# Four-layer graph network on one core: the scatters of layers 1 and 3 become one 128x128 matmul per slot tile

## Chip, core and metric

The kernel runs on one core of one Trainium2 chip. The metric is the device time of one execution in microseconds. The time before is the median of three executions, 5735.22 us, with 5725.06 us the lowest and 5747.24 us the highest.

## What is computed

A graph of 12,500 nodes and 200,000 edges, sorted by destination, passes through four layers. Each layer's result is added to its input and normalised over the 96 features of a node. Cut to the parts that move data over the edges:

```python
x = _layernorm(x + L0(x))   # mean over the edges into a node of x[src], two weight matrices
x = _layernorm(x + L1(x))   # twice: segment_sum((x @ W0 + b0)[src], dst), joined with x @ W1 + b1, times W2, divided by its std
x = _layernorm(x + L2(x))   # attention with 8 heads: exp(clip(sum(K[src] * Q[dst] * E(edge_attr)))) weighs V[src]
x = _layernorm(x + L3(x))   # softmax over the edges into a node: ex = exp(m), sum(ex * m) / sum(ex), then one matrix
```

So each layer gathers a row for every edge by its source and sums the rows by destination. L1 does this twice (depth 2), and L3 sums two quantities for each edge.

## The kernel before

The nodes are 98 tiles of 128. Edges are handled in two ways.

For the first destination tiles (`NS` = 72 tiles in layers 0 and 1, `NS3` = 64 tiles in layer 3) edges are placed in *slots*: each destination tile has `SQ` = 25 slot tiles of 128 slots, and a slot tile is made of four *granules* of `GR` = 32 slots, each of which draws its rows from one source tile. Two one-hot matrices in fp8 belong to a destination tile: `ohT` (source node by slot) and `ohd` (slot by destination node). A slot tile is worked off in three steps:

- *gather* (L1389): four matmuls, one for each granule, each with 128 rows and 32 columns of weights, write the 128 gathered rows into PSUM (`rows1`, `rows2`). A gathered row has `W` numbers: 192 in layers 0 and 1 (a value as two fp16 halves), 384 in layer 3;
- *copy* (L1392): ScalarE or VectorE copies them to SBUF as fp16 (`msg1`, `msg2`);
- *scatter* (L1399): four matmuls, each with 32 columns of `ohd` as weights and the same copied rows as moving operand, add to the 32-partition quarters of one accumulator `acc`, over the 25 slot tiles of a destination tile.

For the remaining destination tiles the rows are fetched straight from DRAM by GpSimd's indirect DMAs, 128 rows each (L1334, into a ring of `rows_e` tiles), and summed by one matmul per edge tile and destination tile, with a one-hot matrix `ones_e` of 128x128 that VectorE makes (L1315, L1320). The helper `by_edges` does this, and its `take(d)` issues the 32 matmuls of a destination tile.

The program has five parts in time. The first (L0, `first_sums`, with its own gather and scatter at L1251 and L1265) also builds the one-hot matrices and stores them. Two calls of `whole_pass` follow, one for each depth of L1, then the attention (`attention`, L1560 to L1700), then a third call of `whole_pass` for L3. A call of `whole_pass` goes through its slot tiles in groups of `5 * R` (10 in L1, 5 in L3, as `R = 4 * D // W`): it gathers a group in three pieces, two copied by ScalarE and one by VectorE, then scatters the group before, and after each group takes from `by_edges` its proportional share. When four destination tiles are complete a stage function runs (`l1_stage` with transposes at L747 and matmuls at L1463 or L1511; `l3_stage` with L1747 to L1777 and matmuls at L1767).

This is the order in which the code calls the steps. The order in which instructions stand on each engine is made from it by a scheduler that has its own costs for the instructions; inside an engine they run in that order. In `whole_pass` PSUM holds two `acc` buffers, one buffer of `rows1` and two of `rows2`. SBUF holds four buffers each of `msg1` and `msg2`, three of each one-hot matrix, and a ring of 16 (L1) or 13 (L3) `rows_e` tiles of four edge tiles each.

Calls of `whole_pass`: `whole_pass(rest, tabs_d[1 + i], ...)` for i = 0, 1 inside `passes()`, and `whole_pass(at_3, ex_d, ...)` after `attention()`. Together they scatter 2 x 72 x 25 = 3,600 slot tiles of 192 columns and 64 x 25 = 1,600 of 384 columns.

Of the kernel before, what the change touches and what calls it, by code (L numbers as in the profile page):

```python
# [23 lines left out]
P = 128  # L24
# [491 lines left out]
GR = 32  # L516
NG = 4
SQ = 25
# [23 lines left out]
def gnn_fast(  # L542
# [4 lines left out]
    nc = tc.nc  # L547
# [630 lines left out]
    def reload(work, d, bufs=3):  # L1178
        o = work.tile([P, SD], FP8, name="ohT0", bufs=bufs)
        nc.sync.dma_start(o, ohT_d[d])  # L1180
        ohd = work.tile([P, SQ, P], FP8, name="ohd", bufs=bufs)
        nc.sync.dma_start(ohd.rearrange("p q e -> p (q e)"), ohd_d[d])
        return o, ohd

    def load_table(pool, table):

        pieces, at = new_table(pool, table.shape[1], F16)
        for k, t in enumerate(pieces):
            (nc.sync, nc.scalar)[k % 2].dma_start(t, rows(table, k * CT, t.shape[1]))
        return at  # L1190
# [10 lines left out]
    def gather_spares(pool, table, d):  # L1201

        t = pool.tile([P, table.shape[1]], F16, name="spare", bufs=4)
        nc.gpsimd.indirect_dma_start(
            out=t, out_offset=None, in_=table,
            in_offset=bass.IndirectOffsetOnAxis(ap=spare_2[:, d // 2 : d // 2 + 1], axis=0),
        )
        return t

    def granule(at, ohs, sp, q, j, half=0):  # L1210

        if q == SQ - 1 and j < 2:
            c = half * SPARE + j * GR
            return ident_h[:, c : c + GR], sp
        s = NG * q + j - (2 if q == SQ - 1 else 0)
        return ohs[:, q * P + j * GR : q * P + (j + 1) * GR], at(s)
# [131 lines left out]
    def whole_pass(of, table, done, rest_done, at=None):  # L1348

        ns = of[0]  # L1350
        W = table.shape[1]
        R = 4 * D // W
        items = [(d, q) for d in range(ns) for q in range(SQ)]
        got, acc = {}, {}
        with ExitStack() as c2:
            tabp = c2.enter_context(tc.tile_pool(name="e_tab", bufs=1))
            work = c2.enter_context(tc.tile_pool(name="e_work", bufs=2))
            msgp = c2.enter_context(tc.tile_pool(name="e_msg", bufs=4))
            psum = c2.enter_context(tc.tile_pool(name="e_psum", bufs=1, space=PSUM))
            at = at or load_table(tabp, table)  # L1360
            sp = {}

            def ask_spares(d):
                if d < ns:
                    sp[d] = sp[d + 1] = gather_spares(tabp, table, d)

            ask_spares(0)
            ask_spares(2)
            others = by_edges(of, msgp, psum, work, table, rest_done, 16 if W == 2 * D else 13)
            next(others)  # L1370
            made = 0

            def fetch(d):
                if d < ns:
                    if d % 2 == 0:
                        ask_spares(d + 4)
                    got[d] = reload(work, d)

            def gather(now, banks, engine):

                n = len(now) // R
                ps = psum.tile([P, n, 512], F32, name=f"rows{n}", bufs=n)
                m = msgp.tile([P, n, R * W], F16, name=f"msg{n}")
                for i, (d, q) in enumerate(now):
                    if q == 0:
                        fetch(d + 1)
                    for j in range(NG):
                        a, b = granule(at, got[d][0], sp[d], q, j, d % 2)
                        nc.tensor.matmul(  # L1389
                            ps[j * GR : (j + 1) * GR, i // R, i % R * W : (i % R + 1) * W], a, b, start=True, stop=True  # L1390
                        )
                (nc.scalar.copy if engine else nc.vector.tensor_copy)(m, ps[:, :, : R * W])  # L1392
                return [(d, q, m[:, i // R, i % R * W : (i % R + 1) * W]) for i, (d, q) in enumerate(now)]

            def scatter(d, q, m):
                if q == 0:
                    acc[d] = psum.tile([P, 512], F32, name="acc", bufs=2)
                for j in range(0, P, GR):
                    nc.tensor.matmul(  # L1399
                        acc[d][j : j + GR, :W], got[d][1][:, q, j : j + GR], m, start=(q == 0), stop=(q == SQ - 1)  # L1400
                    )
                if q == SQ - 1:
                    done(work, psum, d, acc.pop(d))
                    got.pop(d)
                    sp.pop(d)

            fetch(0)
            waiting = []
            for i in range(0, len(items), 5 * R):
                now = []  # L1410
                for b0, b1, scalar in ((0, 1, True), (1, 3, True), (3, 5, False)):
                    now += gather(items[i + b0 * R : i + b1 * R], b1 - b0, scalar)
                for w in waiting:
                    scatter(*w)
                waiting = now
                while made * len(items) < i * 4 * (NB - ns):
                    next(others)
                    made += 1
            for w in waiting:
                scatter(*w)  # L1420
            for _ in others:
                pass
# [491 lines left out]
```

## Time and profile before

| | |
|---|---|
| median of three executions | 5735.22 us |
| the profiled execution | 5735.91 us |
| its span (first to last instruction) | 5733.9 us |
| mean granted TensorE clock | 0.773 |
| TensorE matmuls busy (PE) | 4175.5 us, 73%, 72,859 instructions |
| TensorE weight loads busy (PEld) | 3370.6 us, 59%, 72,859 instructions |
| VectorE (DVE) / ScalarE (ACT) / GpSimd (POOL) busy | 4365.7 / 2727.9 / 3866.0 us |
| L1399, the scatters of the change | 756.2 us of PE busy time, 20,800 matmuls |
| L1389, the gathers of the same passes | 796.5 us, 20,384 matmuls from the tables |
| the two passes of L1 | about 1480 to 2125 us and 2125 to 2800 us of the span |
| the pass of L3 | about 4866 to 5734 us |

Busy times of an engine are the union of its instructions, and matmuls are pipelined: an instruction's own duration (277 ns on average at L1399) is much longer than the distance to the next. "issue" as the reason of an idle time means that the engine waited for no semaphore that the profile shows. In rows of instructions, `128*32` is rows by columns of the array in use, and `xN` a count.

### The profile page before, as it was taken

How to read it: one execution, taken by the hardware profiler on the slowest of the kernel's cores; microseconds unless marked ns; L12 is line 12 of the kernel's file. 1: busy time of each engine (PE TensorE's matmuls, PEld its weight loads, DVE VectorE, ACT ScalarE, POOL GpSimd, SP SyncE). 2: the span in 40 equal slices, each digit the busy share in tenths (PEclk: the TensorE clock that was granted, in tenths of full speed). 3: DMA queues.
4: the chain of work that ended last, by engine and by line, in shares of the span. 5: the costliest groups of instructions: out<-in, count | busy, mean ns of one | idle time of the engine just before them, and what ended most of it. 6: DMA issues, size and time to landing. Idle time of an engine off the chain costs nothing. (4 is left out here: it accounts for less than half of the span.)

```text
span 5733.9 us, 175104 instructions
## 1 busy us (share of the span) xinstructions
PE 4175.5 (73%) x72859; PEld 3370.6 (59%) x72859; DVE 4365.7 (76%) x10305; ACT 2727.9 (48%) x5420; POOL 3866.0 (67%) x3587
## 2 busy tenths in 40 slices
PE   4657766676678877787667677667667666899998
PEld 2545555555567666666466666566666665566665
DVE  7589999998466656666578888888888787677777
ACT  1445555556344434444444545544554454455454
POOL 0267676777577747776277777777777776776663
PEclk7677877888899989999765656655665565999999
DMA  4556666665655645666455555555555554455553
GB/s 103 150 179 198 190 202 199 199 198 177 162 162 166 167 130 161 175 177 173 131 156 159 159 158 161 159 160 159 161 159 161 157 158 131 140 155 149 143 145 90
DMA packets 670059, 920.37 MB, mean 161 GB/s; under 512 B 398170, under 2 KB 463437, under 8 KB 669253
## 3 DMA queue, kind: packets, MB, share of 16 engines
q1 hardware_dynamic: 503350, 624.83, 34.9%
q0 software_dynamic: 147648, 277.89, 19.3%
q8 instruction: 573, 9.39, 0.7%
q10 hardware_dynamic: 18255, 6.35, 0.5%
q14 instruction: 233, 1.91, 0.1%
HBM read 775.87 MB, written 132.81 MB: 158 GB/s over the span
## 5 line engine op out<-in xcount | busy, mean ns | idle before, releaser
L1334 POOL DMA_INDIRECT rows_e<-tab_d,cols x1257 | 1556.3, 1238 | 472.6 <-issue 289.8
L1560 POOL DMA_INDIRECT kv<-kv_d,cols x1563 | 1546.3, 989 | 484.6 <-issue 380.2
L1392 ACT CAST msg<-rows 128x384 f16<-128x384 f32 (+1 forms) x1360 | 820.2, 639 | 784.1 <-PE rows L1389 758.9
L1652 PE MATMUL acc<-mh,ohe 128*128 128x208 f16 x3115 | 561.5, 353 | 623.4 <-DVE ohe L1638 621.5
L1392 DVE CAST msg<-rows 128x768 f16<-128x768 f32 x680 | 649.5, 955 | 387.6 <-PE rows L1389 373.2
L1389 PE MATMUL rows<-tab,ohT 128*32 128x192 f16 (+1 forms) x20384 | 796.5, 277 | 155.4 <-issue 51.8
L1399 PE MATMUL acc<-msg,ohd 128*32 128x192 f16 (+1 forms) x20800 | 756.2, 277 | 70.5 <-issue 65.2
L1652 PEld LDWEIGHTS <-ohe 128*128 128x128 bf16 x3115 | 359.0, 129 | 758.4 <-DVE ohe L1638 702.9
L1389 PEld LDWEIGHTS <-ohT 128*32 128x32 fp8e4 x20384 | 515.0, 98 | 327.6 <-issue 253.1
L1598 PE MATMUL ep<-w_e,attr 97*128 97x96 f32 x3126 | 690.5, 396 | 5.0 <-DVE s L1606 4.2
L1334 POOL DMA_INDIRECT rows_e<-ex_d,cols x547 | 530.6, 970 | 215.5 <-issue 138.7
L1598 PEld LDWEIGHTS ep<-w_e,attr 97*128 97x128 f32 x3126 | 660.8, 311 | 13.4 <-DVE s L1606 4.6
L1399 PEld LDWEIGHTS <-ohd 128*32 128x32 fp8e4 x20800 | 520.8, 99 | 186.4 <-issue 110.0
L1618 ACT ACTIVATE ex<-sc 128x32 f32<-128x32 f32 x391 | 89.6, 229 | 935.4 <-DVE sc L1610 913.1
L1320 PE MATMUL acc<-rows_e,ones_e 128*128 128x192 f16 (+2 forms) x3532 | 464.4, 282 | 84.0 <-DMA rows_e<-tab_d,cols 30.1
L1255 ACT CAST msg<-rows 128x768 f16<-128x768 f32 x600 | 361.3, 640 | 306.2 <-PE rows L1251 283.4
L1606 DVE TENSOR_TENSOR s<-ep,kv 128x384 f32<-128x384 f32 x391 | 217.6, 557 | 310.7 <-DMA kv<-kv_d,cols 230.4
L1320 PEld LDWEIGHTS <-ones_e 128*128 128x128 bf16 x3532 | 338.2, 117 | 189.4 <-issue 98.7
L1265 PE MATMUL acc<-msg,ohd 128*32 128x193 f16 x7200 | 332.8, 287 | 132.2 <-ACT msg L1255 124.7
L1251 PE MATMUL rows<-tab,ohT 128*32 128x192 f16 x7056 | 336.5, 286 | 34.8 <-DVE ohT L1174 12.6
L1638 DVE TENSOR_SCALAR ohe<-wide,within 128x256 bf16<-128x256 bf16 x1563 | 359.5, 314 | 0.0
L1031 DVE TENSOR_TENSOR_SCAN cnt<-cb,run,sb 128x2048 bf16<-128x2048 bf16 (+1 forms) x73 | 324.6, 4447 | 3.7 <-DMA cb<-crow 3.6
(703 smaller groups left out, 7252.9 us busy)
## 6 DMA issues: line engine op xcount, KB each, us to landing
ohT<-ohT_d SPq DMA_DIRECT2D x208, 400.0 KB
ohd<-ohd_d SPq DMA_DIRECT2D x208, 400.0 KB
attr<-cols_edge_attr_dram SPq DMA_DIRECT2D x390, 192.0 KB
bc<-rowd SPq DMA_DIRECT2D x72, 800.0 KB
qb<-qrow SPq DMA_DIRECT2D x97, 512.0 KB
sb<-srow SPq DMA_DIRECT2D x72, 512.0 KB
cb<-crow SPq DMA_DIRECT2D x72, 512.0 KB
ohd_d<-ohd SPq DMA_DIRECT2D x72, 400.0 KB
```

The source lines that it names most:

```text
L1251: nc.tensor.matmul(ps[j * GR : (j + 1) * GR, i // R, i % R * W : (i % R + 1) * W], a, b, start=True, stop=True)
L1255: nc.scalar.copy(m[:, : n * R, :W].rearrange("p (b r) w -> p b r w", r=R), ps[:, :n, : R * W].rearrange("p b (r w) -> p b r w", r=R),)
L1265: nc.tensor.matmul(acc[d][j : j + GR, : W + 1], got[d][1][:, q, j : j + GR], m, start=(q == 0), stop=(q == SQ - 1))
L1320: nc.tensor.matmul(acc[:, : W + count], ones[:, :, i], rows_of[u][:, i, : W + count], start=(t + i == first), stop=(t + i == last),)
L1334: nc.gpsimd.indirect_dma_start(out=m[:, i, :W], out_offset=None, in_=table, in_offset=bass.IndirectOffsetOnAxis(ap=rest_src[:, t : t + 1], ...
L1389: nc.tensor.matmul(ps[j * GR : (j + 1) * GR, i // R, i % R * W : (i % R + 1) * W], a, b, start=True, stop=True)
L1392: (nc.scalar.copy if engine else nc.vector.tensor_copy)(m, ps[:, :, : R * W])
L1399: nc.tensor.matmul(acc[d][j : j + GR, :W], got[d][1][:, q, j : j + GR], m, start=(q == 0), stop=(q == SQ - 1))
L1560: nc.gpsimd.indirect_dma_start(out=kv[:, i, :], out_offset=None, in_=kv_d, in_offset=bass.IndirectOffsetOnAxis(ap=cols[:, t0 + i : t0 + i ...
L1598: nc.tensor.matmul(ep[:, i, :], a[:, i * P : (i + 1) * P], w_e, start=True, stop=True)
L1638: nc.vector.tensor_scalar(o[:, i], wide, within[:, t0 + i : t0 + i + 1], None, op0=ALU.is_equal)
L1652: nc.tensor.matmul(acc[d].rearrange("p t w -> p (t w)"), ohe[:, i, k * P : (k + 1) * P], m[:, i].rearrange("p t w -> p (t w)"), start=(t = ...
```

## The change

In `whole_pass` the four scatter matmuls of a slot tile, one for each 32-column group, become one matmul with the whole 128x128 block of `ohd` as weights, which writes all 128 partitions of `acc`. The gathers in the same passes still use 32 columns at a time, and `first_sums` keeps its four scatters.

```diff
             def scatter(d, q, m):
                 if q == 0:
                     acc[d] = psum.tile([P, 512], F32, name="acc", bufs=2)
-                for j in range(0, P, GR):
-                    nc.tensor.matmul(
-                        acc[d][j : j + GR, :W], got[d][1][:, q, j : j + GR], m, start=(q == 0), stop=(q == SQ - 1)
-                    )
+                nc.tensor.matmul(acc[d][:, :W], got[d][1][:, q, :], m, start=(q == 0), stop=(q == SQ - 1))
                 if q == SQ - 1:
                     done(work, psum, d, acc.pop(d))
```

## Prediction

> **What bounds the kernel now.** I read the page first, then the engines' busy time by part of the program, the groups of instructions of each pass by form, and the timeline of TensorE inside the passes. The profiled execution took 5735.91 us, 2.0 us more than its span and 0.7 us more than the median, so sums are made against 5735.9 and carry over to the median less 0.7. A measurement of this kernel can tell about 0.5% (29 us) from no change.
>
> ```profile
> span 5733.9 us, 175104 instructions
> PE 4175.5 (73%) x72859; PEld 3370.6 (59%) x72859; DVE 4365.7 (76%) x10305; ACT 2727.9 (48%) x5420; POOL 3866.0 (67%) x3587
> ...
> q8 instruction: 573, 9.39, 0.7%
> ```
>
> No engine bounds the whole. By part (engines' busy us and counts, granted clock, DMA share, GB/s):
>
> ```profile
> 0.00:1480.00 1480.00, 956.31 (x18293) 744.18 (x18293) 1265.23 (x2768) 717.99 (x1334) 870.41 (x534) 0.77 0.59 179
> 1480.00:2125.00 645.00, 500.70 (x15685) 433.36 (x15689) 374.00 (x785) 273.83 (x539) 446.36 (x461) 0.92 0.56 156
> 2125.00:2800.00 675.00, 518.31 (x15347) 416.34 (x15335) 438.31 (x949) 300.20 (x669) 441.57 (x450) 0.94 0.58 163
> 2800.00:4866.00 2066.00, 1409.50 (x9394) 1260.36 (x9394) 1654.38 (x4612) 1012.73 (x2140) 1546.86 (x1564) 0.59 0.55 158
> 4866.00:5734.00 868.00, 790.72 (x14153) 516.40 (x14152) 633.76 (x1193) 423.16 (x741) 560.83 (x579) 0.97 0.48 136
> ```
>
> Rows two, three and five are the changed passes. In L3 PE is busy 791 of 868 us. In L1 it is busy 78%, and POOL's 461 operations matter. The groups of the first pass of L1 (first three lines) and of L3 (last four):
>
> ```profile
> L1334 POOL DMA_INDIRECT rows_e<-tab_d,cols x423 | 409.9, 969 | 129.6 <-issue 111.2 <-PE rows L1389 6.1 <-DMA rows_e<-tab_d,cols 5.2
> L1389 PE MATMUL rows<-tab,ohT 128*32 128x192 f16 x7174 | 220.9, 255 | 50.8 <-issue 24.3 <-DMA ohd<-ohd_d 9.8 <-DVE msg L1392 6.6
> L1399 PE MATMUL acc<-msg,ohd 128*32 128x192 f16 x7252 | 213.1, 256 | 39.1 <-issue 39.1
> ...
> L1334 POOL DMA_INDIRECT rows_e<-ex_d,cols x547 | 530.6, 970 | 215.5 <-issue 138.7 <-PE acc L1320 56.7 <-PE rows L1389 15.2
> L1389 PE MATMUL rows<-tab,ohT 128*32 128x384 f16 x6252 | 356.9, 329 | 40.6 <-ACT msg L1392 20.6 <-DVE msg L1392 18.2
> L1399 PE MATMUL acc<-msg,ohd 128*32 128x384 f16 x6400 | 339.4, 328 | 5.3 <-DVE msg L1392 5.3
> L1320 PE MATMUL acc<-rows_e,ones_e 128*128 128x384 f16 x1075 | 191.6, 330 | 19.2 <-DMA rows_e<-ex_d,cols 18.5 <-DVE ones_e L1315 0.6
> ```
>
> In L3 POOL waits 56.7 us for PE's `acc`: it is ahead, and PE sets the pass. In the first pass of L1 POOL waits for hardly anything but its own issue, 0.3 us after each 0.97 us operation; 461 of them need 585 of the 645 us, so POOL sets the pace and PE barely keeps up. In the second pass POOL waits 15.8 us for `acc`, so PE leads there, by little.
>
> **What a slot tile costs in either form.** TensorE alone, in L3 and then L1 (start, us, count):
>
> ```profile
> 5101.56 0.67 PE L1399 MATMUL acc<-msg,ohd 128*32 128x384 f16 x12
> 5102.05 0.35 PE L1389 MATMUL rows<-tab,ohT 128*32 128x384 f16 x4
> 5102.33 0.84 PE L1320 MATMUL acc<-rows_e,ones_e 128*128 128x384 f16 x4
> 5103.10 0.35 PE L1389 MATMUL rows<-tab,ohT 128*32 128x384 f16 x4
> ...
> 1627.15 0.59 PE L1389 MATMUL rows<-tab,ohT 128*32 128x192 f16 x17 [0.65 <-issue]
> 1627.49 1.07 PE L1399 MATMUL acc<-msg,ohd 128*32 128x192 f16 x40
> 1628.32 1.07 PE L1389 MATMUL rows<-tab,ohT 128*32 128x192 f16 x40
> 1629.14 0.83 PE L1399 MATMUL acc<-msg,ohd 128*32 128x192 f16 x31
> 1631.17 0.42 PE L1399 MATMUL acc<-msg,ohd 128*32 128x192 f16 x9 [1.20 <-issue]
> ...
> 1661.36 2.83 PE L1320 MATMUL acc<-rows_e,ones_e 128*128 128x192 f16 x32
> ```
>
> The 12 scatters of 5101.56 are three slot tiles, and the next group starts 0.49 us later: 0.163 us a slot tile. The full matmuls of 5102.33 take 0.84 us for four; less 0.33 us for the last one's own length, 0.17 us each. In L1 ten slot tiles take 0.83 us (1627.49 to 1628.32), and 32 full matmuls (2.83 - 0.25) / 31 = 0.083 us each. So the four column groups already run side by side, and four of them cost what one full matmul costs. **The change saves no streaming time.** That is the first step, and it denies the change its plainest gain.
>
> **What is added: changes of shape.** From the four gathers at 5102.05 to the full matmul is 0.28 us instead of 0.163: +0.12. The four full ones lose another 0.03, as the first weights of the new shape load uncovered. Their last starts at 5102.33 + 0.84 - 0.33 = 5102.84, and the next gathers at 5103.10: 0.26, so +0.10. There and back costs 0.25 us, 0.12 us a change. The Trainium skill (TensorEngine Tiling, Tiling Modes) has it as a rule that changing the tiling mode, not only the tile, drains TensorE; the rows agree, and it gives no price.
>
> In the built programs' orders on PE, the first stage and the attention are the same instructions in the same order. The three passes go from 196, 264 and 172 changes between 32-column and wider matmuls to 459, 559 and 875: in L3 395 from gather to scatter and 359 back, as its 1,600 scatters stand mostly in runs of five. Added are 263, 295 and 703, times 0.12: 32, 35 and 84 us of TensorE time.
>
> **What is removed: instructions.** Every slot tile loses three weight loads and three matmuls, 5,200 x 6 = 31,200 of PE's 145,718. Their time was shared with the fourth, so they cost only where instructions run short. There they do: at 1627.15 and 1631.17 TensorE stands still inside a run, waiting for "issue". Between the two stand 17 + 40 + 40 + 31 = 128 matmuls with as many loads, and the page's instruction queue q8 moved 9.39 MB in 573 packets, 145,718 / 573 = 254 instructions to a packet. I read this as PE running out of fetched instructions: 256 of them last 32 x 0.083 = 2.7 us but came after 4.0 us. The PE rows of L1 put 39.1 + 24.3 = 63 us on issue in the first pass and 26.1 + 27.5 = 54 us in the second; those of L3 none, where 256 instructions last 32 x 0.163 = 5.2 us. After the change a group of L1 is 80 instructions of gather and 20 of scatter in 0.83 + 0.83 + 0.25 = 1.9 us, so 256 last 4.9 us, longer than 4.0. The bounds are nothing saved and all 117 us; near the upper end, I take 85%: 54 and 46 us.
>
> **The sum.** First pass of L1: 32 - 54 = -22 us for PE, but POOL's 585 us stand, and PE can win only part of the 60 us around them: -10. Second pass: 35 - 46 = -11, kept, since POOL waits there. L3: +84, on the engine that sets the pass. Some of it falls where PE waits anyway: its matmul rows wait 40.6 + 5.3 + 18.5 = 64 us for copies and rows, and a PE 10% slower finds these sooner ready. I take a third, 20: +64. No other queue is moved past anything that counts; SP's and POOL's work is the same in number. Together +43: 5735.9 + 43 = 5779, **5778 us** against the median. Its own range goes from L3 covered by half of those waits (84 - 32 - 21 = +31) to nothing covered and half of the stalls left (84 + 67 - 58 = +93): 5766 to 5828.
>
> **Rivals.**
> *Covered drains, faster.* If changes of shape fall where PE waits for copies, rows or instructions anyway, L1 shows only the removed stalls, -10 (POOL) and -46, and L3 84 - 64 = +20: -36, 5699 us. It decides from the point where a change costs L3 less than (56 - 29) / 703 = 0.04 us. For it: 64 us of waits in L3. Against: PE is some 95% busy between 5000 and 5650 us, and L3's waits lie in bursts around its stages, the changes in every group.
> *They cancel.* L3 at half its price, +42, and L1 at -21: +21, 5756 us.
> *The stalls stay.* If a fetch is late because of what other queues move (DMA share 0.56), not because PE is quick, L1 pays 67 and gains nothing: 67 + 84 = +151, 5886 us; cover could take 20 off. Against it: L3, at the same DMA share within 0.1, has none.
> *The quarter matmuls are not quite parallel.* If each group of four cost more than one full matmul, the change would save on all 5,200 slot tiles. A run of 20 in L3 takes 1.00 us; less 0.33 and four distances of 0.163, 0.02 us remain, and a run of 12 (0.67) leaves the same 0.01 to 0.02, so it is paid once in a run. Paid on every slot tile it would be 5,200 x 0.02 = 104 us, 32 of them in L3, and in L1, with POOL's pace, about 20 of the rest: 43 - 52 = -9, 5726 us. The Trainium skill (TensorE: Matmul & The Clock Gate, Part 3) gives such a span, the matmul's length and about 4 ns for each further tile; by it 12 ns x 5,200, an estimate of 62 us, would be saved in place of 104. The rows speak against paying it on each.
>
> **How the numbers follow.** Forecast 0.54, stalls stay 0.08: slower 0.62. They cancel 0.18, not quite parallel 0.05: within 0.5%, 0.23. Covered drains: faster 0.15. The range leaves out the far half of the faster case and nearly all of the stalls' case: 5705 to 5835.
>
> **What would show it.** Right: in L3 PE's distances inside runs stay 0.163 us, weight loads at both ends of each scatter run wait about 0.1 to 0.2 us for issue, and the pass grows by some 64 us; the issue waits of 1.2 us in L1 are nearly gone and POOL's 1.27 us beat fills the first pass as before; L0 and attention keep their length. Wrong: L3 grows by under 30 us (cover), or L1 still shows stalls inside runs of gathers.

## The result, and the profile after

The changed kernel is faster: 5694.09 us in the median of four executions (5689.09 to 5701.9) against 5735.93 us for the kernel before beside it, a ratio of 0.9929, with a 95% interval of 0.9912 to 0.9946. On another chip, in four executions, it took 5690.28 us where the kernel before took 5735.41 us, a ratio of 0.9914 (0.9897 to 0.9932). The prediction was 5778 us, slower than before, with a range from 5705 to 5835: the time moved the other way and lies below the range. The profiled execution took 5689.09 us.

From the page of the changed kernel, the lines that answer to those shown of before:

```profile
span 5687.3 us, 143915 instructions
PE 4272.4 (75%) x57259; PEld 3233.5 (57%) x57259; DVE 4359.9 (77%) x10305; ACT 2734.2 (48%) x5420; POOL 3876.0 (68%) x3587
...
q8 instruction: 451, 7.39, 0.5%
```

TensorE is busy 97 us *longer* (4272.4 against 4175.5) with 15,600 matmuls fewer, and the kernel is 47 us shorter: time that was idle has gone. By part of the program (the columns are those of the same view of before: stretch, length, busy us and count of PE, PEld, DVE, ACT and POOL, granted clock, DMA share, GB/s):

```profile
0.00:1480.00 1480.00, 964.10 (x18293) 749.43 (x18293) 1263.46 (x2764) 717.76 (x1334) 878.03 (x533) 0.76 0.60 179
1480.00:2100.00 620.00, 512.53 (x10173) 411.54 (x10177) 373.22 (x787) 273.36 (x536) 441.20 (x459) 0.91 0.60 160
2100.00:2735.00 635.00, 543.77 (x10072) 400.95 (x10061) 433.64 (x956) 307.83 (x679) 447.97 (x454) 0.94 0.65 177
2735.00:4805.00 2070.00, 1416.21 (x9550) 1259.43 (x9551) 1662.98 (x4618) 1019.44 (x2147) 1557.78 (x1573) 0.59 0.57 158
4805.00:5687.00 882.00, 835.74 (x9187) 412.13 (x9183) 626.56 (x1181) 415.76 (x726) 551.03 (x570) 0.97 0.48 132
```

From here on a pass is measured from its first scatter to its last, read from the start times in the trace. The first pass of L1 went from 611 to 586 us, the second from 657 to 600, L3 from 844 to 871: -25, -57 and +27. L0 and the attention are within 5 us of what they were. The groups of the first pass of L1 (two lines) and of L3 (three), by form:

```profile
L1334 POOL DMA_INDIRECT rows_e<-tab_d,cols x420 | 404.6, 963 | 128.0 <-issue 108.8 <-DMA rows_e<-tab_d,cols 9.1 <-PE rows L1389 5.8
...
L1398 PE MATMUL acc<-msg,ohd 128*128 128x192 f16 x1800 | 190.1, 253 | 0.0
...
L1334 POOL DMA_INDIRECT rows_e<-ex_d,cols x541 | 523.9, 968 | 237.1 <-issue 134.3 <-PE acc L1320 80.9 <-PE rows L1389 16.4
...
L1389 PE MATMUL rows<-tab,ohT 128*32 128x384 f16 x6118 | 343.6, 330 | 12.7 <-ACT msg L1392 11.8 <-DVE msg L1392 0.2
L1398 PE MATMUL acc<-msg,ohd 128*128 128x384 f16 x1570 | 323.1, 329 | 0.0
```

In L1 the 39.1 us that the scatters waited for issue are gone, as predicted. In L3 TensorE waits less for copies (by its waits over the whole pass 18.0 us, 38.8 before), and POOL waits 80.9 us for `acc` where it waited 56.7: TensorE sets that pass more firmly than before. TensorE alone, in L1 and then in L3 (start, us, count):

```profile
1626.40 1.01 PE L1389 MATMUL rows<-tab,ohT 128*32 128x192 f16 x40
1627.34 1.00 PE L1398 MATMUL acc<-msg,ohd 128*128 128x192 f16 x10
1628.27 1.01 PE L1389 MATMUL rows<-tab,ohT 128*32 128x192 f16 x40
...
5054.02 1.00 PE L1389 MATMUL rows<-tab,ohT 128*32 128x384 f16 x20
5054.95 0.99 PE L1398 MATMUL acc<-msg,ohd 128*128 128x384 f16 x5
5055.87 0.35 PE L1389 MATMUL rows<-tab,ohT 128*32 128x384 f16 x4
```

A group of L1 (ten slot tiles gathered, ten scattered) takes 1628.27 - 1626.40 = 1.87 us with no stall in it; 1.9 was predicted. A group of L3 takes 5055.87 - 5054.02 = 1.85 us where ten distances of 0.163 make 1.63: 0.22 us for the drains (the time lost at a change of shape) there and back, where 0.25 was predicted. These mechanisms are all there, which points to something that the sum did not hold.

### The profile page after: what moved, and what is told of

Its sections match the earlier page's. It is cut to its first block, busy times and chain, and to the rows that moved or that the text cites. A ratio compares the mean times of both kernels' runs of the same rounds, so it can differ in the third digit from the quotient of the medians.

```text
span 5687.3 us, 143915 instructions
## 1 busy us (share of the span) xinstructions
PE 4272.4 (75%) x57259; PEld 3233.5 (57%) x57259; DVE 4359.9 (77%) x10305; ACT 2734.2 (48%) x5420; POOL 3876.0 (68%) x3587
## 5 line engine op out<-in xcount | busy, mean ns | idle before, releaser
L1334 POOL DMA_INDIRECT rows_e<-tab_d,cols x1257 | 1576.9, 1255 | 457.8 <-issue 290.4
L1389 PE MATMUL rows<-tab,ohT 128*32 128x192 f16 (+1 forms) x20384 | 780.7, 277 | 61.9 <-ACT msg L1392 18.6
L1398 PE MATMUL acc<-msg,ohd 128*128 128x192 f16 (+1 forms) x5200 | 708.3, 276 | 1.4 <-issue 1.3
L1389 PEld LDWEIGHTS <-ohT 128*32 128x32 fp8e4 x20384 | 432.0, 97 | 366.6 <-issue 314.5
L1398 PEld LDWEIGHTS <-ohd 128*128 128x128 fp8e4 x5200 | 413.1, 99 | 241.8 <-issue 183.8
```

Source lines behind the costliest of these rows:

```text
L1334: nc.gpsimd.indirect_dma_start(out=m[:, i, :W], out_offset=None, in_=table, in_offset=bass.IndirectOffsetOnAxis(ap=rest_src[:, t : t + 1], ...
L1389: nc.tensor.matmul(ps[j * GR : (j + 1) * GR, i // R, i % R * W : (i % R + 1) * W], a, b, start=True, stop=True)
L1398: nc.tensor.matmul(acc[d][:, :W], got[d][1][:, q, :], m, start=(q == 0), stop=(q == SQ - 1))
```

## The experiments: the matmul, or the order

The change does two things at once. It replaces four instructions by one, and it gives the scheduler another cost for the scatter, so that all five engines get another order of instructions. The prediction took the new order from the built program, but only to count changes of shape in it. One theory: *the form* of the matmul makes the result (fewer stalls in L1, drains that are better hidden). The other: *the order* makes the gain, because waits inside TensorE's order become shorter, and the form costs about what was predicted. To part them, the order of one kernel was forced on the other, instruction by instruction on every engine in the three passes, by dependencies that carry no semaphore (`...` stands for lines left out, here and below):

```diff
+    for engine in (ET.PE, ET.DVE, ET.Activation, ET.Pool, ET.SP):
+        own = [i for i in traced[a:b] if i.engine == engine and type(i).__name__.startswith("Inst")]
+        ...
+        for step in given[at : at + len(own)]:
+            k += step
+            if last is not None:
+                tc.add_manual_dep(own[k], last.name, mybir.DependencyInfo(
+                    mybir.DependencyClass.NoSync, mybir.DependencyReason.DATA), reason="order")
+            last = own[k]
```

`one_old` is the changed kernel in the order of before; `four_new` is the kernel before (four matmuls, kept together) in the order of after. The traces bear the edit out: VectorE, ScalarE and GpSimd have the same operations in the same order in `one_old_c` as in the kernel before, and in `four_new_d` as in the changed kernel. Beside them the change was made in one layer alone, the scheduler free to order (`l1_only`, shown against the changed kernel; `l3_only` has `R == 1` in place of `R == 2`):

```diff
-                nc.tensor.matmul(acc[d][:, :W], got[d][1][:, q, :], m, start=(q == 0), stop=(q == SQ - 1))
+                G = P if R == 2 else GR
+                for j in range(0, P, G):
+                    nc.tensor.matmul(
+                        acc[d][j : j + G, :W], got[d][1][:, q, j : j + G], m, start=(q == 0), stop=(q == SQ - 1)
+                    )
```

Some of these runs were on two chips on which the kernel before takes 8058 and 8066 us; they are told first and kept apart.

**On the slower chips.** Kernel `one_old`:

> One 128x128 matmul per slot tile, but every engine in the three passes is held to the order of instructions of the kernel before. Instruction supply and cover (the theory): the time comes from fewer instructions in L1 and from drains that L3's waits cover, whatever the order: 5685 to 5705 us, the two L1 passes 40 us or more shorter together, L3 about 27 us longer. Order (rival): the gain is the scheduler's new order, which puts the stages' transposes later behind the scatters; without it the waits stay: L1 shorter by no more than 30 us together, L3 longer by 60 to 80, 5765 to 5785 us.

Kernel `four_new`:

> Four quarter matmuls per slot tile as before, but every engine in the three passes is held to the order of the changed kernel. Supply and cover: the instructions are as many as before and the stalls stay, 5725 to 5745 us, issue waits of PE in L1 near 117 us. Order: the waits at the transposes go and there are no drains, so L1 shorter by 30 us and L3 by 50: 5645 to 5670 us.

The change in layer 1 alone, and in layer 3 alone:

> One matmul per slot tile in the two passes of L1, four in L3. If the parts add up (both theories): L1 as in the changed kernel, 75 to 85 us shorter, L3 as before: 5655 to 5670 us. If the slower L3 of the changed kernel came from something that it inherits from L1: L3 stays 27 us longer, 5690 us.

> Four matmuls in L1, one in L3. If the parts add up: L1 as before, L3 27 us longer: 5755 to 5770 us. If the drains of L3 are wholly covered when it starts from the state that the old L1 leaves: 5735 us.

Measured against 8058.47 us: `one_old_order` 8014.54 (ratio 0.9945, 0.9925 to 0.9965), `four_new_order` 8018.41 (0.9961, 0.9947 to 0.9974), `l1_only` 7950.23 (0.9871, 0.9849 to 0.9894), `l3_only` 8089.97 (1.0056, 1.0036 to 1.0076). The form alone and the order alone both gain here, by some 40 us each. Numbers of us for a pass can't be held against these runs, since the passes of L1 take about 1,000 us in place of 600. The sign by layer holds: layer 1 gains, layer 3 loses. On the second of these chips, with one kernel more (strict turns in L3, below):

> One 128x128 matmul per slot tile in the order of the kernel before (looked at part by part this time). Supply and cover: the two passes of L1 about 75 us shorter together than before's 1268, L3 about 27 us longer than 844. Order: L1 30 us shorter at most, L3 60 to 80 us longer. Both at work, each with about half, as the slower chip showed it: L1 40 us shorter, L3 15 to 20 us longer.

> Four quarter matmuls in the order of the changed kernel. Supply and cover: L1 1268 us as before with issue waits near 117 us, L3 844 us. Order: L1 30 us shorter, L3 50 us shorter. Both: L1 35 to 40 us shorter, L3 10 us longer.

> One matmul in L1, four in L3. If the parts add up, L1 1186 us as in the changed kernel and L3 844 us as before: 5660 us in all.

> The changed kernel with one thing more: in L3 the groups of five gathers and of five scatters are held in strict turns, which takes the changes of shape in L3 from 876 to 715. If each drain stands on PE's path at 0.105 us, L3 is 17 us shorter than the changed kernel's 871: 854. If the drains lie in waits, it stays at 871; if the fixed turns make PE wait for copies, it is longer.

Against 8065.7 us, one execution each: 8029.79, 8024.0, 7974.11 and 7959.99 us. The first three repeat the times above within 24 us. The copies take as long here as in `l1_only_c`, the same kernel on a faster chip (800 ns on ScalarE and 955 on VectorE for 128x768, against 800 and 954); TensorE is what differs. Its waits in `l1_only_b` over the whole span (engine, line, waited for, us, times, longest):

```profile
PE rows L1389 <- issue: 605.0, 750, 3.2
...
PE acc L1400 <- issue: 298.4, 391, 2.5
```

750 and 391 times it stood still without a semaphore, for 0.8 us on average; in the profile of before the same two lines have some 50 such stalls each. With fewer instructions in L1 the kernel gains there (`l1_only`), but with fewer in L3 it still loses (`l3_only`). What slows these chips is open, and no result below rests on them.

**On chips where the kernel before takes 5731 to 5749 us.**

> One matmul per slot tile in the order of the kernel before, for a chip where before takes 5735 us; by parts, before being L1 611 + 657 and L3 844, after 586 + 600 and 871. Supply and cover, whatever the order: L1 1186 as after, L3 871. Order alone: L1 1240 or more, L3 905 to 925. Both: L1 near 1225 (stalls gone, drains added, the transposes' waits of the old order still there), L3 875 to 890.

> Four matmuls per slot tile in the order of the changed kernel, on such a chip. Supply and cover: issue waits of PE in L1 stay near 117 us, L1 1268, L3 844. Order alone: L1 1186 or less, L3 790 to 800. Both: L1 near 1235 with the stalls still there, L3 830 to 845.

> One matmul in L1, four in L3, on such a chip. If the parts add up: L1 1186, L3 844, 5660 us, faster than both kernels.

> The changed kernel with strict turns of five gathers and five scatters in L3 (715 changes of shape instead of 876), on such a chip. If each drain stands on PE's path at 0.105 us: L3 854 instead of 871. If the drains lie in waits: 871. On the slower chip L3 was 25 us shorter than with the new order and one matmul.

Measured, against 5737.32 us: `one_old_c` 5719.23, `four_new_c` 5656.42, `l1_only_c` 5656.89 (four executions, 0.9863, 0.9847 to 0.988), `l3_turns_c` 5687.22; all but `l1_only_c` are single executions. `one_old_c` came as expected for both effects at work (L1 1219 us in its two passes, L3 881). In `four_new_c` the order is worth more than that: L1 took 1201 us, between the 1186 expected for the order alone and the 1235 for both, and L3 828. `four_new` was run again, for an interval:

> Four matmuls for every scatter, in the order of the changed kernel on every engine: an interval for the effect of the order alone. If the order makes the gain, 5656 us again (ratio 0.984 to 0.988) and layer 3 near 828; if the matmul's form makes it and the earlier look was a chance, 5700 or more.

It took 5660.23 us, a ratio of 0.9872 (0.9854 to 0.989). **The order alone, with not one scatter changed, gains more than the change itself.** The passes, in us:

| | first pass of L1 | second pass of L1 | L3 |
|---|---|---|---|
| four matmuls, order of before (before) | 611 | 657 | 844 |
| one matmul, order of before (`one_old_c`) | 590 | 629 | 881 |
| four matmuls, order of after (`four_new_d`) | 592 | 613 | 827 |
| one matmul, order of after (after) | 586 | 600 | 871 |

The passes of the kernels before and after in a second profile of each agree with this table within 3 us. With four matmuls the order is worth -19, -44 and -17; with one, -4, -29 and -10. In the order of before the form is worth -21, -28 and +37, and in the order of after -6, -13 and +44. So the two do not simply add. Order first and then form, it is -80 and +25 us over the three passes; form first and then order, -12 and -43. Both effects shorten the first pass of L1, and together they do little more than either. GpSimd takes 576 to 581 us there from its first transfer to the end of its last in all four kernels; what shrinks is what TensorE has left to do after it, from 37 us before to 19 with either effect and 16 with both.

Holding an order does not by itself change the time visibly: `split96` (below) has the scatters of L3 and their order as in the changed kernel, but held, and its L3 takes 874 us, against 871 and 873 in the two profiles of the changed kernel.

*What the order takes away* stands in the waits of TensorE in the second pass of L1. Before:

```profile
PE rows L1389 <- issue: 27.5, 20, 3.4
PE acc L1399 <- issue: 26.1, 22, 2.9
PE rows L1389 <- DVE msg L1392: 20.1, 29, 1.9
PE tp L747 <- DVE xg L775: 19.3, 17, 1.4
...
PE tp L1511 <- DVE q L755: 12.9, 43, 0.6
PE rows L1389 <- ACT msg L1392: 9.9, 17, 1.1
```

The same scatters in the order of after (`four_new_d`):

```profile
PE acc L1400 <- issue: 32.2, 21, 3.9
...
PE rows L1390 <- issue: 17.3, 20, 1.7
PE rows L1390 <- DVE msg L1393: 13.1, 26, 1.3
PE tp L1513 <- DVE q L755: 7.1, 36, 0.2
...
PE tp L747 <- DVE xg L775: 5.0, 13, 0.8
...
PE rows L1390 <- ACT msg L1393: 0.2, 1, 0.2
```

The rows of that pass, before and then `four_new_d` (stretch, length, busy us of PE first):

```profile
2121.00:2778.00 657.00, 512.47 (x15394) 414.26 (x15387) 425.23 (x912) 296.95 (x656) 443.21 (x452) 0.95 0.60 167
...
2104.00:2717.00 613.00, 504.14 (x15399) 409.87 (x15391) 418.25 (x912) 301.52 (x656) 446.48 (x451) 0.96 0.64 179
```

The stalls on issue are nearly the same, 53.6 and 49.5 us. What shrank most are waits on semaphores: the transposes of `l1_stage` (L747) and its matmuls for VectorE's `xg` (19.3 to 5.0) and `q` (12.9 to 7.1), and the gathers for copies (30.0 to 13.3). That is 37 us less; waits for fetched rows grew by 8, and in all TensorE's idle time fell by 36 of the 44 us and its busy time by 8. In the order of before a transpose stands in TensorE's queue before its input is ready, and everything behind it waits. In the order of after it stands later: by the two traces 80 of the 98 transposes of `xg` have more gathered and scattered slot tiles ahead of them, in the median of all by 17, and none has fewer.

In the first pass of L1 the order's 19 us are another matter. Its rows, before and then `four_new_d`, and the stalls on issue of `four_new_d`:

```profile
1486.00:2096.00 610.00, 481.94 (x15371) 418.29 (x15363) 361.82 (x751) 264.11 (x517) 435.91 (x450) 0.94 0.57 157
...
1487.00:2079.00 592.00, 469.00 (x15411) 411.90 (x15404) 361.75 (x751) 266.16 (x518) 435.79 (x450) 0.96 0.59 162
...
PE acc L1400 <- issue: 47.8, 31, 4.5
PE rows L1390 <- issue: 29.3, 24, 2.5
```

The stalls on issue are longer there, 77 us against 63, and some 10 us come from TensorE's busy time: 469 and 472 us in the two profiles of `four_new` on these chips against 482 and 480 in those of before, at a granted clock of 0.95 to 0.96 against 0.94. Why the clock differs, and why the scheduler's order comes out better when it counts a scatter at one matmul, was not tested.

*What the form does* stands in L3, in the row of each pass (stretch, length, busy us of PE first). The kernel before:

```profile
4866.00:5710.00 844.00, 782.08 (x14112) 510.72 (x14111) 620.07 (x1150) 419.94 (x733) 560.83 (x579) 0.98 0.49 140
```

`four_new_d`:

```profile
4810.00:5636.00 826.00, 775.77 (x14100) 506.49 (x14096) 617.37 (x1150) 418.62 (x732) 562.17 (x579) 0.98 0.50 143
```

`one_old_c`:

```profile
4813.00:5694.00 881.00, 841.52 (x9309) 418.17 (x9309) 620.01 (x1150) 418.38 (x731) 559.63 (x579) 0.98 0.46 133
```

After:

```profile
4791.00:5662.00 871.00, 841.28 (x9310) 412.22 (x9310) 620.61 (x1150) 420.85 (x732) 560.15 (x579) 0.98 0.49 135
```

In either order TensorE is busy some 841 us with one matmul and 776 to 782 with four: +59 and +66 us by the form. Its idle time in the pass falls from 62 to 40 us in the old order and from 50 to 30 in the new. So the drains cost 59 to 66 us, some 20 us of them fall into waits that were there anyway, and the rest lengthens L3. The order itself is worth -17 us in L3 with four matmuls, 12 of it in idle time.

**Strict turns in L3** (`l3_turns_c`): a dependency without a semaphore makes each group's gathers and scatters follow one another whole, which brings the changes of shape in L3 from 875 to 715.

```diff
+            def turn(own):
+                if R == 1 and own:
+                    ...
+                            tc.add_manual_dep(
+                                i, ends[0].name,
+                                mybir.DependencyInfo(mybir.DependencyClass.NoSync, mybir.DependencyReason.DATA), reason="turns",
```

L3 took 870 us, where 854 was expected if each drain stands on TensorE's path and 871 if the drains lie in waits; the kernel took 5687.22. The row of its L3:

```profile
4791.00:5661.00 870.00, 827.09 (x9297) 421.17 (x9294) 620.18 (x1147) 415.77 (x730) 558.84 (x579) 0.98 0.47 135
```

TensorE is busy 14 us less than in after, as 160 changes at 0.09 us should give, and idle 13 us more. So neither reason holds as it was put: the drains did stand on TensorE's path, and the turns brought waits in their place. It says the same again: removing a cost from TensorE's order is worth only what the new order does not give back in waits.

**Are the stalls really a matter of instructions?** The kernel before and after once more, and `split96`: after's order, but in L1 each scatter is two matmuls of 96 columns. The streaming is the same and TensorE has 7,200 instructions more, counting the loads. Shown against the changed kernel:

```diff
-                nc.tensor.matmul(acc[d][:, :W], got[d][1][:, q, :], m, start=(q == 0), stop=(q == SQ - 1))
+                H = D if R == 2 else W
+                for h in range(0, W, H):
+                    nc.tensor.matmul(
+                        acc[d][:, h : h + H], got[d][1][:, q, :], m[:, h : h + H], start=(q == 0 and h == 0), stop=(q == SQ - 1 and h + H == W)
+                    )
```

> The kernel before, unchanged, for its trace on a chip of the kind that ran the experiments (8058 us there instead of 5736). Supply: the 2300 us more lie in stalls of PE without a semaphore, in L1, L3 and the attention alike. Otherwise: they lie in transfers or in one engine's slower clock.

> The changed kernel, unchanged, on such a chip. If the two effects that the held orders showed there add up (fewer instructions and the new order, in L1 50 and 42 us, in L3 22 and 11 us the other way): 8058 - 92 + 33 = 8000 us, with the bounds of a part's scatter on these chips some 20 us either way. Supply alone: as with the old order, 8015 us. On a chip like the first one: 5694 us.

> The changed kernel with its own order of instructions on every engine; in L1 each scatter is two matmuls of 96 columns with the same weights instead of one of 192: 7,200 PE instructions more, the same changes of shape. Supply: L1 longer than with one matmul, by 15 to 35 us on the two passes on a chip like the first one, by more where stalls are more frequent (7,200 of the 21,600 instructions that the change took out of L1: a third of its gain there, or more). Order and drains alone: L1 within 10 us of the changed kernel's.

The three were meant for one of the slower chips and ran on one like the first, so what makes the others slow was not seen. Before and after repeated themselves: 5748.66 us in one execution of before, 5690.28 for after, with passes of L1 of 609 and 659 against 586 and 600. `split96` took 5686.93 us with passes of 585 and 599 us, so it lost nothing: the expected loss of 15 to 35 us missed. The waits of TensorE in its two passes of L1:

```profile
PE rows L1390 <- issue: 10.0, 12, 2.7
```

That is 10 us of issue in both passes together, where the kernel before has 117. A group of `split96` is 80 instructions of gather and 40 of scatter in 1.89 us, so 256 last 256 / 120 x 1.89 = 4.0 us, just the 4.0 us at which they came in the kernel before. This fits a supply that costs nothing until it is asked for more than 256 instructions in 4.0 us; the point itself was not measured more closely. That the number of instructions is the cause is not shown by it: a scatter of four 128x128 matmuls, each over 48 of the 192 columns, has as many instructions as before; it would have tested that and was not run.

**The parts put together.** If order and form are separate, one matmul in L1 and four in L3, all in the order of after, should take the best of each. `best` is the edit of `l1_only` with the order of after held:

> The order of the changed kernel, instruction by instruction on every engine; in layer 1 the scatter is one matmul, in layer 3 four. By the theory of two separate effects (a better order, worth -80 us with four matmuls, and one matmul, worth -15 us in layer 1 and +43 in layer 3 in that order): layer 1 586 + 600 us as in the changed kernel, layer 3 828 as with four matmuls in that order, together 5736 - 80 - 15 = 5641 us, 5630 to 5655. By the rival that the orders found by the scheduler are only noise around a common level and the matmul's form alone counts (layer 1 one matmul 586 + 600, layer 3 four 844): 5657, the time of the kernel with one matmul in layer 1 alone in its own order. If it lands above 5665 neither holds. On a chip on which the kernel before takes about 8058 us the first theory expects layer 3 below that of the kernel before by 5 to 15 us and layer 1 below by 75 us, the second layer 3 level.

It took 5643.69 us (5631.51 to 5645.69) against 5731.35 us, a ratio of 0.984 (0.9819 to 0.9861), with passes of 588, 601 and 826 us, where the sum of the two effects said 586, 600, 828 and 5641. The row of its L3:

```profile
4790.00:5617.00 827.00, 776.88 (x14113) 506.81 (x14113) 617.94 (x1151) 419.07 (x732) 561.91 (x579) 0.98 0.50 143
```

The rival, that the scheduler's orders are noise around one level, expected 844 us for L3 and 5657 in all. It falls: L3 takes 826 us in the order of after, held, and 843 in `l1_only_c`, which has the same instructions there in an order that the scheduler found for itself. `best` is the fastest kernel of this study, 1.6% below before and 0.7 to 0.9% below the changed kernel. Without any forced order `l1_only_c` gets 1.4%.

## Why the prediction was wrong

**The step that failed** is in the part on what is added: the new order on TensorE was read for its number of changes of shape and for nothing else, and the sum then says "No other queue is moved past anything that counts". The three passes had another order on every engine, and that order is worth -71 us with four matmuls (5660.23 against 5731.35; -80 by the three passes) and -43 us by the passes with one. The term was not mis-sized but missing. The rows that it acts on were before the reader: the gathers of L3 waited 38.8 us for copies, and in the second pass of L1 the same trace had TensorE's transposes and stage matmuls waiting 32.2 us for VectorE's `xg` and `q`, which the prediction never listed.

The terms that were in the sum fared better, when each is held against the same order (after against `four_new_d`):

- *Streaming.* Four matmuls in column groups cost what one costs: right. In after a run of five full scatters lasts 0.99 us, which is the last one's 0.33 and four distances of 0.165. The commonest distance from one scattered slot tile to the next in L3 is 162 or 163 ns with four matmuls (`four_new_d`) and with one, so the rival that the quarter matmuls are not quite parallel finds no support.
- *A change of shape.* 0.12 us was taken. The commonest distances in L3 of after, from the first matmul of one slot tile to that of the next, are 268 ns from a gather to a scatter and 256 ns back, against 162: 106 and 94 ns, and TensorE's busy time rose by 65.5 us for 716 changes, 0.091 us each. In L3 84 us should have been 64. In the two passes of L1 busy time rose by 28 and 25 us, where 32 and 35 were taken. The drain that the Trainium skill states as a rule (TensorEngine Tiling (Array Packing), Tiling Modes) is there; its price here is these 0.09 to 0.11 us.
- *Cover in L3.* A third of the waits, 20 us, was taken: right, 20 and 22 us in the two orders. So the form costs L3 37 us in the order of before and 44 in that of after, where the sum had +64, and the difference is the price of the drain (in the order of before also their number, 654 where 703 was taken).
- *Stalls in L1.* Gone, as predicted: after has 1.0 us of them in the first pass and 3.1 in the second.
- *POOL's pace.* Right in the order of after: the form is worth -6 us in the first pass (-10 predicted) and -13 in the second (-11 predicted), though 77 and 50 us of stalls are taken away in them. In the order of before it is -21 and -28, twice what was predicted. In the first pass of after the time went into the drains, 28 us, and into waits for transfers that POOL issues:

```profile
PE rows L1389 <- DMA spare<-tab_d,spare: 40.0, 9, 8.6
PE acc L1320 <- DMA rows_e<-tab_d,cols: 27.2, 31, 1.7
```

Those are the first two waits of TensorE in the first pass of L1 of after; in `four_new_d` they are 8.9 and 14.9 us, so 43 us went there.

Together the form alone was forecast at +43 us. In the order of after, against `four_new_d`, it is +24 to +33 us by the ratios (0.9914 and 0.9929 against 0.9872): the sign of the forecast, 10 to 20 us less. In the order of before it is -18 us (`one_old_c`, one execution; -12 by the passes), against the forecast's sign. So the terms hold only where the order is the new one, for which the changes of shape were counted, and the order itself, which was not forecast, turned the sum round. The prediction named L3 longer by under 30 us as a sign of cover; it came, with 27 us, but at a fixed order L3 pays 37 to 44, and the order takes 10 to 17 back.

**The rivals.** *Covered drains* gave 5699 us, close to the 5694 measured, but that is luck: in a fixed order L3 pays 37 to 44 us and not 20, and of the 82 us that L1 gains the form has 19 or 49, by whether it is taken after the order or before it. *They cancel* had the form's parts best, L3 at +42 and L1 at -21: in the order of after they are +44 and -19. As a forecast of the whole, 5756 us, it is out, because the order is missing from it too. *The stalls stay* is out: they are gone.

## What to carry to other kernels

Where a scheduler orders the program, a change of one instruction's cost changes the order of everything, and the new order can be worth more than the instruction: hold the order of either kernel fixed, and cost the two separately, in both orders, since the two need not add. When the new order is known before the run, read where each waiting instruction stands against its producer (here transposes in TensorE's queue behind VectorE), not only how many instructions of a kind there are. An engine relieved on a pass that another engine paces returns its time as waits for that engine.

## What the runs showed of the hardware

TensorE's stalls without a semaphore in L1 are not in proportion to the number of its instructions: 200 instructions in 3.7 us (after, two groups of L1) went with 4 us of them in the two passes, 240 in 3.8 us (`split96`) with 10 us, and 320 in 3.3 us (`four_new_d`, two groups at 1.66) with 127 us. Where between the last two they set in was not measured.

Four matmuls in four column groups take no longer than one of the full width, 162 to 163 ns for a slot tile of 384 columns and 82 to 83 ns for one of 192. A change between 32-column and full-width matmuls costs 0.09 to 0.11 us.

On the two slower chips TensorE stood still for about 0.8 us at a time, in `l1_only_b` 750 times before a gather, where the kernel before has 43 such stalls on its chip, and 349 times at `qp` of the attention, which has none there. The granted clock was 0.70 to 0.72 against 0.77 or more, a factor of some 1.1, which does not by itself explain 8058 against 5735 us, a factor of 1.4.
